# A finished tile's sums and products behind the thresholding pass, a small product and half of a ratio to VectorE

## The chip, the cores and the metric

The kernel runs on one core of a Trainium2 chip. A core has five engines with a queue of instructions each: TensorE (PE; its weight loads are shown as PEld), VectorE (DVE), ScalarE (ACT), GpSimd (POOL) and SyncE (SP), which issues most of the DMAs. Each engine works through its queue in order and waits on semaphores for the others. The metric is the device time of one execution in microseconds, as a median of several runs, here 1416.24 us (1415.47 to 1416.34 in 3 runs).

## The reference

A layer of a graph network on 3327 nodes with 256 features, all in float32. The input is normalized and cut at zero; then there are two steps, each with a fixed diffusion and an attention whose rows keep only the largest probabilities up to a mass of 0.9.

```python
def _top_p_attention(X, W1, W2, W3):
    q = X @ W1.T @ W2.T
    k = X @ W3.T
    probs = jax.nn.softmax(q @ k.T / TAU, axis=-1)
    idx = jnp.argsort(-probs, axis=-1)
    sp = jnp.take_along_axis(probs, idx, axis=-1)
    cs = jnp.cumsum(sp, axis=-1)
    keep_sorted = cs - sp < TOP_P
    mask = ...  # keep_sorted, put back in place
    A = probs * mask
    return A / jnp.maximum(A.sum(-1, keepdims=True), 1e-12)

R = S + jnp.eye(N)
R = R / R.sum(-1, keepdims=True)
for n in range(2):
    A = _top_p_attention(Xa, W1, W2, W3)
    Xf = R @ Xf
    Xa = A @ Xa
    Z = Z + Xf @ U1[n].T + Xa @ U2[n].T
h = X + Z
out = x + (h - mean) / sqrt(var + 1e-5) * ln_g + ln_b
```

## The kernel before

The 3327 nodes are 26 tiles of 128 rows (NT). A first part makes the keys, the products with the weights and the first lists; then come the two steps of the reference, called step 1 and step 2 here (`step` 0 and 1 in the code), tile after tile. At the end a flag says whether every row's cut was proved; if not, a second, slow kernel (`search_graph_layer`) would run. It doesn't for this input.

For one tile of 128 rows the work is:

- `weights`: TensorE makes the logits against all 3328 keys, ScalarE takes the exponential into an array `e` (128x3328).
- `measured_twice` (step 2; `measured_once` in step 1): a guess of the cut that is refined. ScalarE passes over all of `e` three times in step 2 (`through`, the tile `ja`, L633), and each pass ends in one sum per row. Between the passes small columns (128x1, the tile `g`, `col(k)` in the code) are worked out on VectorE, ScalarE and GpSimd. L685 and L686 follow the first pass; L690 to L692 on GpSimd make columns 14, 10 and 8; L699 and L700 follow the second pass; L707 to L712 on GpSimd make the ratio that ends in column 11, which ScalarE's L714 needs. L716 and L717 make the guess, column 16.
- `settle`: VectorE keeps what lies below the guess (L731, the tile `w`, 128x3328), takes the eight largest of each of 20 segments (L736), sorts out the largest in rounds (L743, L745), finds the cut (L750 to L755), masks `e` in place with the row sum beside it (L765) and takes the reciprocal (L766). L767 multiplies two arrays of 48 (40 in step 1) columns into `cum`, and L769 takes its maximum for the proof. L767 is on VectorE in step 1 and on GpSimd in step 2.
- `Sums`: TensorE transposes the masked `e` (L810), ScalarE copies it (L812), TensorE multiplies it with the features (L824).
- `spread`: the diffusion by a few gathered rows (`refetch` issues five gathers on GpSimd, L903; TensorE L911), ended by VectorE's L1086 into `s`.
- `finish` (step 2): L935 on VectorE joins the two sums, L458 and L459 take mean and variance, GpSimd makes the inverse deviation (L465, L466) and L943, ScalarE normalizes (L950), GpSimd adds the offset to the input rows `xr` (L945), multiplies (L951) and adds (L952), and SyncE writes the tile out (L955).

Order: each of these is a Python generator, and a table written by hand says when each takes its next part. Every tile's turn `i` has seven slots; a letter in a slot's string takes one part of one generator: `m` and `n` are the measuring of the next tile and the rest of the one before it, `d` and `c` the same for `settle`, `s` is `spread`, `f` is `finish`, `w` is `weights`, `g` the gathers. The order in which instructions are issued by the program is then fixed on TensorE, ScalarE and VectorE, and in step 2 on GpSimd, by dependencies that need no semaphore. So a part that is moved in the text moves in its engine's queue.

In step 2 GpSimd's queue for a tile is: L707 to L712, L945, L951, L952, L767, L677 and L678 (the next tile's first columns, which wait for ScalarE's L676), five gathers, L690 to L692, L465, L466, L943, L697, L698. On VectorE L717 is followed by L731, L732, L769, ten of L736, L935, L685, L686, L1086, ten more of L736, L458, L459, three rounds, L699, L700, three rounds, L750 to L755, L765, L766, L716, L717.

Of the kernel before, what the change touches and what calls it, by code (L numbers as in the profile page):

```python
# [14 lines left out]
ALU = mybir.AluOpType  # L15
# [7 lines left out]
NT = (N + P - 1) // P  # L23
# [321 lines left out]
def guess_graph_layer(ctx, tc, x, adj, w1t, w2t, w3t, u1t, u2t, ln_g, ln_b, out, flag):  # L345
# [323 lines left out]
    def measured_twice(r):  # L669
        e, ms = r["e"], r["ms"]  # L670

        col = guessed(r, small.tile([P, 18], F32, tag="g", name="g"))
        S.activation(col(1), col(0), AF.Exp, scale=-1.0, bias=con(5))
        S.activation(col(11), col(2), AF.Square, bias=con(4))  # L676
        G.tensor_scalar(col(11), col(11), ms(5), ms(6), ALU.mult, ALU.add)  # L677
        G.tensor_scalar(col(5), col(1), OFFSET[1], None, ALU.mult)  # L678
        yield
        oa = small.tile([P, 3], F32, tag="oa", name="oa")  # L680
        through(e, AF.Relu, col(9), -1.0, oa[:, 0:1])
        yield
        through(e, AF.Sign, col(9), -1.0, oa[:, 1:2])
        yield
        V.tensor_scalar(col(3), oa[:, 1:2], float(NP), col(9), ALU.add, ALU.mult)  # L685
        V.tensor_scalar(col(4), col(3), 0.5, oa[:, 0:1], ALU.mult, ALU.subtract)  # L686
        S.activation(col(6), col(4), AF.Ln, scale=col(1), bias=con(2))
        S.activation(col(6), col(6), AF.Exp, scale=col(11))
        S.activation(col(13), col(6), AF.Copy, scale=col(9))
        G.tensor_scalar(col(14), col(13), col(9), 0.25, ALU.add, ALU.mult)  # L690
        G.tensor_scalar(col(10), col(13), col(5), 1.0, ALU.mult, ALU.add)
        G.tensor_scalar(col(8), col(4), col(1), -1.0, ALU.mult, ALU.add)  # L692
        yield
        through(e, AF.Sign, col(13), -1.0, oa[:, 2:3])
        yield
        d1 = col(17)
        G.tensor_scalar(col(0), oa[:, 2:3], NP - 61.0, BIG, ALU.is_gt, ALU.mult)  # L697
        G.tensor_scalar(col(0), r["Z"], 0.035, col(0), ALU.mult, ALU.add)  # L698
        V.tensor_scalar(col(15), oa[:, 2:3], oa[:, 1:2], col(14), ALU.subtract, ALU.mult)  # L699
        V.tensor_scalar(d1, col(15), col(4), 0.0, ALU.add, ALU.max)  # L700

        S.activation(col(2), d1, AF.Abs, scale=col(1), bias=con(1))
        S.activation(col(2), col(2), AF.Ln, scale=0.2, bias=col(10))
        S.activation(col(3), d1, AF.Ln, scale=col(1), bias=con(2))
        S.activation(col(2), col(2), AF.Identity, scale=-1.0, bias=col(3))

        G.tensor_scalar(col(12), col(4), d1, col(1), ALU.subtract, ALU.mult)  # L707
        G.tensor_scalar(col(8), col(8), col(12), None, ALU.mult)
        G.tensor_scalar(col(12), col(12), col(12), 1.0e-12, ALU.mult, ALU.add)
        G.tensor_tensor(col(12), col(12), half[:, 2:3], ALU.pow)  # L710
        G.tensor_scalar(col(12), col(12), col(8), 0.7, ALU.mult, ALU.max)
        G.tensor_scalar(col(11), col(12), 1.5, col(11), ALU.min, ALU.mult)  # L712
        yield
        S.activation(col(3), col(2), AF.Exp, scale=col(11))  # L714
        yield
        V.tensor_scalar(col(6), d1, col(0), BIG, ALU.is_lt, ALU.mult)  # L716
        V.tensor_scalar(col(16), col(3), col(13), col(6), ALU.mult, ALU.add)  # L717
# [7 lines left out]
    def settle(step, t, r):  # L725
        e, col, Z = r["e"], r["col"], r["Z"]
        n = 8 * ROUNDS[step]
        d2 = small.tile([P, 1], F32, tag="d2", name="d2")
        need = small.tile([P, 1], F32, tag="need", name="need")
        w = scan.tile([P, NP], F32, tag="w", name="w")  # L730
        V.scalar_tensor_tensor(w, e, col(16), e, ALU.is_lt, ALU.mult, accum_out=d2)  # L731
        V.tensor_scalar(need, Z, -0.1, d2, ALU.mult, ALU.add)  # L732
        yield
        cand = small.tile([P, NSEG * 8], F32, tag="cand", name="cand", bufs=1)
        for s in range(NSEG):
            V.max(cand[:, 8 * s : 8 * s + 8], w[:, s * SEG : min(NP, (s + 1) * SEG)])  # L736
            if s in (NSEG // 2 - 1, NSEG - 1):
                yield
        at = lambda k: rec[:, step, k, t : t + 1]
        V.tensor_reduce(at(0), cand.rearrange("p (s k) -> p s k", k=8)[:, :, 7], AX.X, ALU.max)  # L740
        for k in range(ROUNDS[step]):
            b8 = bb[:, 1 + 8 * k : 9 + 8 * k]
            V.max(b8, cand)  # L743
            if k < ROUNDS[step] - 1:
                V.match_replace(cand, b8, cand, 0.0)  # L745
            if k == 2:
                yield
        b = bb[:, 1 : n + 1]
        cum = small.tile([P, TOPK], F32, tag="cum", name="cum", bufs=1)
        V.tensor_tensor_scan(cum[:, :n], bb[:, :n], bb[:, :n], 0.0, ALU.add, ALU.max)  # L750

        dr = small.tile([P, TOPK], F32, tag="dr", name="dr", bufs=1)
        V.tensor_scalar(dr[:, :n], cum[:, :n], need, None, ALU.is_ge)
        V.scalar_tensor_tensor(cum[:, :n], dr[:, :n], BIG, b, ALU.mult, ALU.add)
        V.tensor_reduce(at(1), cum[:, :n], AX.X, ALU.min)  # L755
        yield
        r["ra"] = ra = small.tile([P, 1], F32, tag="ra", name="ra")
        if t in (0, NT - 1):

            rb = small.tile([P, 1], F32, tag="rb", name="rb", bufs=1)  # L760
            for a, b_, r_ in ((0, FIRST, ra), (FIRST, NP, rb)):
                V.scalar_tensor_tensor(e[:, a:b_], e[:, a:b_], at(1), e[:, a:b_], ALU.is_ge, ALU.mult, accum_out=r_)
            V.tensor_tensor(ra, ra, rb, ALU.add)
        else:
            V.scalar_tensor_tensor(e, e, at(1), e, ALU.is_ge, ALU.mult, accum_out=ra)  # L765
        V.reciprocal(ra, ra)  # L766
        (G if step else V).tensor_tensor(cum[:, :n], dr[:, :n], b, ALU.mult)  # L767
        yield
        V.tensor_reduce(at(2), cum[:, :n], AX.X, ALU.max)  # L769


# [162 lines left out]
    def finish(t, y, pa, ra):  # L934
# [7 lines left out]
        nm = small.tile([P, 1], F32, tag="nm", name="nm")  # L942
        G.tensor_scalar(nm, mv[:, 0:1], rstd, -1.0, ALU.mult, ALU.mult)  # L943
        yield
        G.tensor_tensor(xr, xr, bet, ALU.add)  # L945
        if t == NT - 1:
            V.scalar_tensor_tensor(y, y, mv[:, 0:1], gam, ALU.subtract, ALU.mult)
            V.scalar_tensor_tensor(y, y, rstd, xr, ALU.mult, ALU.add)
        else:
            S.activation(y, y, AF.Identity, bias=nm, scale=rstd)  # L950
            G.tensor_tensor(y, y, gam, ALU.mult)  # L951
            G.tensor_tensor(y, y, xr, ALU.add)  # L952
        yield
        h = min(P, N - t * P)
        nc.sync.dma_start(out[t * P : t * P + h], y[:h])  # L955

# [135 lines left out]
    def refetch(t):  # L1092
# [8 lines left out]


    PLAN = (("mdsssa", "mdsssa", "edawwp", "msda", "mpdea", "gdawwq", "emdgq"),
            ("llcmss", "lnms", "lwwnfd", "lcmdsssg", "fmswqdf", "llmdf", "lmwfd"))

    LAST = {NT - 1: ("cfss", "cn", "ndddddd", "sss", "fsf", "f", "f"), NT: ("cf", "v", "", "", "ff", "f", "fv")}
    LATE = (1, 4)
# [122 lines left out]
```

## Time and profile before

| what | value |
|---|---|
| median of 3 runs | 1416.24 us (1415.47 to 1416.34) |
| the profiled execution | 1414.41 us |
| its span in the profile | 1412.7 us |
| granted TensorE clock, mean | 0.973 of full speed |
| busy: PE, DVE, ACT, POOL | 1275.6, 1220.8, 1105.4, 983.1 us |
| step 1 | about 90 to 780 us of the span |
| step 2, from the first full tile to the last | 833 to 1344 us, 23 intervals from mask pass to mask pass |

The profile is one execution. An instruction's line is its place in the code (L765), followed by the engine, the operation, the tile it writes and those it reads, and shapes. In a timeline the first column is the start in us from the span's start and the second the duration in us, from the moment that the engine takes it up; an instruction that is held by something else than a semaphore is shown as long, and the bracket at the end of a line says how long the engine was idle before it and who ended that. A busy share of 90% says little on what sets the time; the waits and the chain that ended last say more.

### The profile page before, as it was taken

To read this page: it belongs to the slowest core of one execution; us is meant where nothing else is said; L and a number is where in the kernel's file an instruction comes from. 1 tells how busy PE (TensorE), PEld (TensorE's weight loads), DVE (VectorE), ACT (ScalarE), POOL (GpSimd) and SP (SyncE) were. 2 spreads that over 40 slices of the span, in tenths; PEclk is the share of its full clock that TensorE was granted. 3 is DMA by queue.
4 is the path that set the end of the run, shared out by engine and by line. 5 is a ranking of instruction groups with operands and counts; after the bars stand their busy time and mean duration, and the time that the engine had idled before them with its cause. 6 is when DMAs were issued, how large, how long until landed. Compare 5 with 4: busy or idle time off the path is not lost.

```text
span 1412.7 us, 22245 instructions
## 1 busy us (share of the span) xinstructions
PE 1275.6 (90%) x6495; PEld 980.1 (69%) x6495; DVE 1220.8 (86%) x3727; ACT 1105.4 (78%) x2423; POOL 983.1 (70%) x1348
## 2 busy tenths in 40 slices
PE   6898999999999999999998479999999999999846
PEld 5545777777777777778786257777777777777745
DVE  6879999999999999998853689999999999999980
ACT  5467887878778787888835689999999999999811
POOL 6214777678667676778853768888888888888721
PEclk9999999999999999999999589999999999999978
DMA  8884454444545454423331211312222122221100
GB/s 273 266 254 127 135 150 130 137 139 141 144 128 147 128 143 144 132 82 91 88 97 49 71 44 54 90 57 79 76 59 87 55 85 59 77 83 53 57 8 22
DMA packets 91203, 149.78 MB, mean 106 GB/s; under 512 B 15265, under 2 KB 58656, under 8 KB 91072
## 3 DMA queue, kind: packets, MB, share of 16 engines
q1 hardware_dynamic: 73616, 105.37, 23.7%
q0 software_dynamic: 16640, 42.69, 11.9%
q8 instruction: 54, 0.88, 0.3%
q14 instruction: 77, 0.63, 0.1%
q10 hardware_dynamic: 816, 0.20, 0.1%
HBM read 120.93 MB, written 27.28 MB: 105 GB/s over the span
## 4 chain that ended last, share of the span: by engine, by line
DVE 51%; PE 25%; ACT 17%; POOL 3%; issue 3%; DMA 1%; SPq 0%; DVEq 0%; POOLq 0%; ACTq 0%
ACT ja L633 11%; PE pa L824 10%; DVE e L765 10%; DVE cand L736 7%; DVE w L731 6%; DVE fm L846 5%; PE pl L600 4%; DVE bb L743 4%; DVE cand L745 4%; PE pt L810 3%; PE pz L988 2%; DVE x L765 2%; ACT eT L812 2%; PE pr L911 1%; ACT e L604 1%
## 5 line engine op out<-in xcount | busy, mean ns | idle before, releaser
L824 PE MATMUL pa<-xw,eT 128*128 128x256 f32 x1352 | 331.1, 387 | 18.6 <-DVE s L935 18.4
L633 ACT ACTIVATE ja<-e,g 128x3328 uint8<-128x3328 f32 x106 | 325.9, 3074 | 0.1
L824 PE MATMUL pa<-x,eT 128*128 128x256 f32 x1352 | 323.7, 381 | 0.0
L824 PEld LDWEIGHTS pa<-xw,eT 128*128 128x128 f32 x1352 | 249.6, 191 | 79.6 <-issue 27.1
L812 ACT COPY eT<-pt 128x512 f32<-128x512 f32 (+1 forms) x364 | 202.1, 556 | 92.9 <-PE pt L810 92.8
L824 PEld LDWEIGHTS pa<-x,eT 128*128 128x128 f32 x1352 | 244.1, 191 | 25.7
L736 DVE MAX8 cand<-w 128x8 f32<-128x168 f32 (+1 forms) x1040 | 251.1, 317 | 0.0
L810 PE MATMUL pt<-ident,e 128*128 128x128 f32 x1144 | 180.6, 278 | 57.9 <-DVE e L765 39.1
L894 POOL DMA_INDIRECT ac<-in_adj,index x130 | 130.2, 1002 | 133.1 <-DVE ms L538 94.9
L903 POOL DMA_INDIRECT xg<-bx,index x130 | 192.4, 1480 | 41.3 <-issue 28.9
L810 PEld LDWEIGHTS pt<-ident,e 128*128 128x128 f32 x1144 | 140.8, 144 | 104.7 <-issue 48.8
L731 DVE SCALAR_TENSOR_TENSOR w<-e,g 128x3328 f32<-128x3328 f32 x44 | 168.9, 3838 | 0.7
L903 POOL DMA_INDIRECT xg<-vx,index x130 | 130.8, 1007 | 45.6 <-issue 33.0
L765 DVE SCALAR_TENSOR_TENSOR e<-e,rec 128x3328 f32<-128x3328 f32 x40 | 156.3, 3907 | 0.7
L911 PE MATMUL pr<-xg,ac 128*128 128x257 f32 (+1 forms) x520 | 139.1, 391 | 11.4 <-DVE s L1086 11.2
L604 ACT ACTIVATE e<-pl 128x832 f32<-128x832 f32 x132 | 112.9, 859 | 36.1 <-PE pl L600 36.0
L911 PEld LDWEIGHTS pr<-xg,ac 128*128 128x128 f32 x520 | 93.9, 195 | 24.9 <-DVE s L1086 11.4
L951 POOL TENSOR_TENSOR s<-s,gam 128x256 f32<-128x256 f32 x25 | 92.5, 3699 | 8.5 <-ACT s L950 8.5
L743 DVE MAX8 bb<-cand 128x8 f32<-128x160 f32 x286 | 92.8, 324 | 6.4
L600 PE MATMUL pl<-after,qT 64*128 64x416 f32 x416 | 96.7, 559 | 0.6 <-ACT qT L528 0.6
L767 POOL TENSOR_TENSOR cum<-dr,bb 128x48 f32<-128x48 f32 x26 | 84.8, 3262 | 15.1 <-DVE rec L755 14.9
L600 PE MATMUL pl<-both,qT 64*128 64x416 f32 x416 | 90.7, 539 | 0.9 <-DVE both L1006 0.9
(259 smaller groups left out, 2197.3 us busy)
## 6 DMA issues: line engine op xcount, KB each, us to landing
at<-in_adj SPq DMA_DIRECT2D x102, 256.0 KB, 3.0
cx<-ac SPq DMA_DIRECT2D x26, 384.0 KB, 2.3
ac<-cx SPq DMA_DIRECT2D x26, 384.0 KB, 3.1
wide<-in_adj SPq DMA_DIRECT2D x10, 832.0 KB, 4.3
e<-in_adj SPq DMA_DIRECT2D x8, 832.0 KB, 5.9
bx<-e SPq DMA_DIRECT2D x26, 128.5 KB, 2.2
own<-bx SPq DMA_DIRECT2D x26, 128.5 KB, 2.9
x<-in_x SPq DMA_DIRECT2D x13, 256.0 KB, 4.7
```

The source lines that it names most:

```text
L600: PE.matmul(pl[:, a, :wd], qT[p, :], keys_of(step, a).rearrange("p a b -> p (a b)")[:, c : c + wd], start=True, stop=True)
L633: S.activation(ja, e, f, bias=guess, scale=sign, accum_out=total)
L731: V.scalar_tensor_tensor(w, e, col(16), e, ALU.is_lt, ALU.mult, accum_out=d2)
L736: V.max(cand[:, 8 * s : 8 * s + 8], w[:, s * SEG : min(NP, (s + 1) * SEG)])
L743: V.max(b8, cand)
L765: V.scalar_tensor_tensor(e, e, at(1), e, ALU.is_ge, ALU.mult, accum_out=ra)
L810: PE.transpose(pt[:, j, :], e[:, (j0 + j) * P : (j0 + j + 1) * P], ident)
L812: S.copy(eT[:, :w, :], pt[:, :w, :])
L824: PE.matmul(self.pa, eT[:, c - 4 * k, :], self.xa[:, j, :], start=c == 0, stop=c == NT - 1)
L894: G.indirect_dma_start(out=ac[:, k, :], out_offset=None, in_=rows, in_offset=bass.IndirectOffsetOnAxis(ap=index[:, t, k : k + 1], axis=0), ...
L903: G.indirect_dma_start(out=xg[:, k, :w], out_offset=None, in_=rows, in_offset=bass.IndirectOffsetOnAxis(ap=index[:, t, k : k + 1], axis=0))
L911: PE.matmul(pr[:, :w], ac[:, k, :], own if k == KT - 1 else xg[:, k, :w], start=k == 0, stop=k == KT - 1)
```

## The change

There are four edits.

1. In `measured_twice` the ratio is worked out in another form. Column 8 is now column 4 less a tenth of `Z` (still one GpSimd instruction). Column 12 is the reciprocal of column 4 less `d1`, by two VectorE instructions, in place of four on GpSimd (a difference with a product, a product, a square with an offset, a power of -1). The last two GpSimd instructions stay.
2. In `settle` the product `cum` is on VectorE in both steps, and it is issued one part later, directly ahead of the maximum that reads it. In step 1 it was on VectorE already.
3. In `finish` the three GpSimd instructions on a finished tile come one part later, so that in GpSimd's queue they stand behind L677 and L678 of the next tile and ahead of the gathers. The writing out, which waits for them, stays behind them. The last tile is as it was.
4. In the table's fifth slot of step 2 `fmswqdf` becomes `fsmwqdf`: on VectorE L1086 comes directly ahead of L685 and L686.

```diff
-        G.tensor_scalar(col(8), col(4), col(1), -1.0, ALU.mult, ALU.add)
+        G.tensor_scalar(col(8), r["Z"], -0.1, col(4), ALU.mult, ALU.add)
...
-        G.tensor_scalar(col(12), col(4), d1, col(1), ALU.subtract, ALU.mult)
-        G.tensor_scalar(col(8), col(8), col(12), None, ALU.mult)
-        G.tensor_scalar(col(12), col(12), col(12), 1.0e-12, ALU.mult, ALU.add)
-        G.tensor_tensor(col(12), col(12), half[:, 2:3], ALU.pow)
+        V.tensor_scalar(col(12), col(4), d1, 1.0e-30, ALU.subtract, ALU.add)
+        V.reciprocal(col(12), col(12))
         G.tensor_scalar(col(12), col(12), col(8), 0.7, ALU.mult, ALU.max)
         G.tensor_scalar(col(11), col(12), 1.5, col(11), ALU.min, ALU.mult)
...
         V.reciprocal(ra, ra)
-        (G if step else V).tensor_tensor(cum[:, :n], dr[:, :n], b, ALU.mult)
-        yield
+        yield
+        V.tensor_tensor(cum[:, :n], dr[:, :n], b, ALU.mult)
         V.tensor_reduce(at(2), cum[:, :n], AX.X, ALU.max)
...
         yield
-        G.tensor_tensor(xr, xr, bet, ALU.add)
         if t == NT - 1:
+            G.tensor_tensor(xr, xr, bet, ALU.add)
             V.scalar_tensor_tensor(y, y, mv[:, 0:1], gam, ALU.subtract, ALU.mult)
             V.scalar_tensor_tensor(y, y, rstd, xr, ALU.mult, ALU.add)
         else:
             S.activation(y, y, AF.Identity, bias=nm, scale=rstd)
+        yield
+        if t < NT - 1:
+            G.tensor_tensor(xr, xr, bet, ALU.add)
             G.tensor_tensor(y, y, gam, ALU.mult)
             G.tensor_tensor(y, y, xr, ALU.add)
-        yield
         h = min(P, N - t * P)
         nc.sync.dma_start(out[t * P : t * P + h], y[:h])
...
-            ("llcmss", "lnms", "lwwnfd", "lcmdsssg", "fmswqdf", "llmdf", "lmwfd"))
+            ("llcmss", "lnms", "lwwnfd", "lcmdsssg", "fsmwqdf", "llmdf", "lmwfd"))
```

## The prediction

> **What bounds the kernel now.** I read the page first: its busy times and the shares of the chain that ended last.
>
> ```profile
> span 1412.7 us, 22245 instructions
> PE 1275.6 (90%) x6495; PEld 980.1 (69%) x6495; DVE 1220.8 (86%) x3727; ACT 1105.4 (78%) x2423; POOL 983.1 (70%) x1348
> DVE 51%; PE 25%; ACT 17%; POOL 3%; issue 3%; DMA 1%; SPq 0%; DVEq 0%; POOLq 0%; ACTq 0%
> ```
>
> VectorE (DVE) leads the chain and GpSimd (POOL) holds only 3% of it, so time taken off GpSimd pays only where GpSimd holds up another engine. Most edits lie in step 2, so next I read who waits there: VectorE's waits from 820 to 1340 us (sum in us, times, longest).
>
> ```profile
> engine line waited for: us in total, times, longest us
> DVE g L685 <- ACT ja L633: 11.0, 22, 0.9
> DVE g L699 <- ACT ja L633: 7.8, 20, 3.4
> ```
>
> Once per tile VectorE waits for each of two ScalarE passes. Following them in time gives one closed loop per tile: first pass (ja) ends, L685 and L686, ScalarE's L687, second pass, L699 and L700, the rest of the candidate rounds, the mask pass L765 (e, 128x3328), TensorE's transposes, ScalarE's copy of them, first pass of the next tile. A tile takes 22.2 us. What is added on this loop adds to every tile; the thresholding pass L731 (w) is beside it, with the wait at L685 as its slack. The timeline of VectorE (start, duration, both in us) shows what GpSimd does to it. First a tile without a collision, then usual ones:
>
> ```profile
> 833.29 3.69 DVE L765 SCALAR_TENSOR_TENSOR e<-e,rec 128x3328 f32<-128x3328 f32 x1
> 837.71 3.68 DVE L731 SCALAR_TENSOR_TENSOR w<-e,g 128x3328 f32<-128x3328 f32 x1
> 844.03 0.47 DVE L935 SCALAR_TENSOR_TENSOR s<-pa,ra,s 128x256 f32<-128x256 f32 x1
> 845.43 0.21 DVE L685 TENSOR_SCALAR g<-oa,g 128x1 f32<-128x1 f32 x1 [0.94 <-ACT ja L633]
> 855.11 4.07 DVE L765 SCALAR_TENSOR_TENSOR e<-e,rec 128x3328 f32<-128x3328 f32 x1
> ...
> 1033.10 4.08 DVE L765 SCALAR_TENSOR_TENSOR x<-x,rec 128x3328 f32<-128x3328 f32 x1
> 1037.91 4.13 DVE L731 SCALAR_TENSOR_TENSOR w<-x,g 128x3328 f32<-128x3328 f32 x1
> 1045.63 0.21 DVE L685 TENSOR_SCALAR g<-oa,g 128x1 f32<-128x1 f32 x1 [0.48 <-ACT ja L633]
> ```
>
> and GpSimd's own timeline beside 1033 us:
>
> ```profile
> 1032.96 0.72 POOL L945 TENSOR_TENSOR xr<-xr,bet 128x256 f32<-128x256 f32 x1
> 1033.66 4.10 POOL L951 TENSOR_TENSOR s<-s,gam 128x256 f32<-128x256 f32 x1
> 1037.84 0.72 POOL L952 TENSOR_TENSOR s<-s,xr 128x256 f32<-128x256 f32 x1
> 1038.52 3.65 POOL L767 TENSOR_TENSOR cum<-dr,bb 128x48 f32<-128x48 f32 x1
> ```
>
> A GpSimd product that started 0.14 us before L765 makes it 4.08 instead of 3.69; one that started 0.07 before L731 makes that 4.13. Over all tiles the delay is about 0.52 us less the head start. The next GpSimd instruction is then held until the pass ends (4.10 and 3.65 for work of 0.72 and 0.26). The tile that starts undelayed at 833.29 lasts 21.82 us to the next L765, against 22.2: the 0.40 is on the loop.
>
> **The change, part by part.** All terms are against the profiled execution, 1414.41 us (span 1412.7 and 1.7 around it), which is 1.83 below the median 1416.24.
>
> *L765 set free.* The three instructions on a finished tile (L945, L951, L952) now stand behind L677 and L678, which wait for ScalarE's L676; that ends some 2 us after L765 starts. GpSimd is idle when L765 starts: 22 tiles times 0.40 = -8.8 us.
>
> *Half of the last ratio to VectorE.* Four GpSimd instructions go (L707 to L710, 0.37+0.29+0.26+0.57); L711 and L712 stay. VectorE gains a subtraction and a reciprocal behind L700, each waiting for the one before. A dependent pair of this form has a pitch of 0.25 (L685 to L686), L700 to an independent successor 0.13, L766's reciprocal to its successor 0.08: 0.25+0.25+0.08-0.13 = 0.45 us, on the loop, because L699 is released by ScalarE and idle time before it cannot be used. 23 pitches times 0.45 = +10.4. The bound below is 0.16+0.08 = 0.24, if the two overlap as independent ones do; above 0.60. I take 0.45, whose rows have the same form. L702 to L705 on ScalarE wait for L700 only and don't move. L692 keeps its one instruction in a new form, 0.25 either way.
>
> [...]
>
> *The sums and products in their new place.* L677 is held by L765 until 0.14 before its end, as other held instructions are; then 0.41 to L678, 0.23 to the sum: 4.17 us after L765's start. L731 starts 4.42 after it (833.29 to 837.71). So the sum is in flight with a head start of 0.25, and L731 is delayed by 0.52-0.25 = 0.27 instead of 0.45. The product is held by L731 and runs when it ends, where the next edit puts a two-input VectorE instruction. The writing out of the tile (SyncE) moves from 5.5 to about 10 us behind L765; behind it in that queue stand x, s, ac and own of later tiles, first used 15 us or more after. GpSimd's five gathers follow the product at about 9.7; today they start at 10.0, held by TensorE. I cost both at nothing; gathers late by over a microsecond would reach L697.
>
> [...]
>
> *cum to VectorE, s in front of L685.* In step 2 cum costs VectorE 0.22 (in step 1 one tile already has the pair adjacent: 724.78 to 725.00), and 0.27 more if the product is in flight: the same pair collides in step 1, where the source view has durations (ns, least, median, most)
>
> ```profile
> L767 DVE TENSOR_TENSOR cum<-dr,bb x26: 179/181/522, 116.3 to 724.8; 128x40 f32<-128x40 f32 x26
> ```
>
> L1086 (0.40) moves from behind L686 to before L685. The slack there without collisions is 845.43-844.43 = 1.00. After: 1.00-0.40-0.22-0.27 (L731)-0.27 (cum) = -0.16, so L685 is late by 0.16 instead of waiting. 23 times 0.16 = +3.7. Bounds: 0 (either collision absent) and 0.34 (L731 delayed by 0.45 as today).
>
> *Irregular tiles.* At 899.5 and 1055.3 gathers came late, and pitches were 22.54 and 23.05; GpSimd now has over 1 us more room: -1.1.
>
> *Step 1.* cum moves five rows back. It leaves a place where it costs 0.10, to one where it costs 0.22 as half of an adjacent pair: 26 times 0.12 = +3.1, on an engine that hardly waits there. At ten tiles it cost 0.44 instead of 0.10, behind L928; the new place is about 1.5 us later, when L928 is over: -3.4. Together -0.3, bounds -3 and +3.
>
> *The start and the end of step 2.* These are the places where GpSimd is waited for.
>
> ```profile
> 811.30 0.29 ACT L714 ACTIVATE g<-g 128x1 f32<-128x1 f32 x1 [0.77 <-POOL g L712]
> ...
> 1350.04 0.20 DVE L769 TENSOR_REDUCE rec<-cum 128x1 f32<-128x48 f32 x1 [1.44 <-POOL cum L767]
> ```
>
> At the start the ratio ends about 1.3 us earlier for tile 0 and 2.1 for tile 1, of which 0.45 comes back in VectorE: -1.6 at 833 us. At the end L731 starts 6.45 after L765; without the wait and the collision it is 3.73 to the reciprocal and 1.03 from there (0.08, cum 0.22, 0.12, 0.30, 0.31) = 4.76: -1.7, less 0.2 for a possible collision: -1.5.
>
> The sum: -8.8+10.4+3.7-1.1-0.3-1.6-1.5 = +0.8 us. On the median: 1417.0.
>
> **The rivals.** About 0.2% (2.8 us) is what a measurement here can tell from no change.
>
> *Faster: the slack holds.* If GpSimd's sum starts after L731 rather than 0.25 before, or cum is not hit, the 3.7 disappears: -2.9. With the two new instructions at 0.30 instead of 0.45 another -3.4: 1410 to 1413.3. For it: the head start of 0.25 is a difference of two chains. Against: the held instruction is released by L765's end, which fixes the order.
>
> *Slower: VectorE becomes the loop at L685.* If L731 is still delayed by 0.45, L685 is 0.34 late, another 0.18 times 23 = +4.1: 1421.1, and with step 1 at its upper bound (+3.3 on mine) 1424.4. It decides from 0.09 of lateness beyond mine in each tile (2.0 us). For it: 0.34 of delay was measured for cum in step 1. Against: L731's delay has always followed the head start.
>
> *It frees nothing: GpSimd is hidden anyway.* Only the loop's 0.45 would then stay; excluded for L765, since the 21.82 pitch is in the trace, and possible if GpSimd's gathers drift until L711 and L712 meet L765: up to 8.8 more, 1425.8.
>
> **How the numbers follow.** Forecast (terms nearly cancel) 0.45; faster rival 0.24; slower rival 0.26; nothing freed 0.05. The forecast's own range is 1413.5 to 1419; towards the rivals 1411 to 1424.5, with about 0.1 beyond each end. Within 0.2% of 1416.24 is 1413.4 to 1419.1: the forecast case, with a little of it lost to each side and a little of the rivals gained. Faster 0.25, same 0.44, slower 0.31.
>
> **What would show it.** In the profile after, step 2: the mask pass at 3.68 in all tiles; the w pass near 3.95; cum near 0.5; no wait left at the L685 of today, one of 0.6 or more at L699; pitch of a tile 22.35 to 22.5; the last w pass 4.8 after the mask pass; ScalarE's L714 not waiting for GpSimd. Step 1: cum 0.18 everywhere. I am wrong if the mask pass still shows 4.08, if the pitch is under 22.2 or over 22.6, or if the gathers start over 1 us later than today.

## The result and the profile after

| | kernel before | changed kernel |
|---|---|---|
| median, same chip, 20 runs each | 1415.91 us (1414.01 to 1417.81) | 1417.85 us (1415.57 to 1421.31) |
| ratio, 95% interval | | 1.0017 [1.0011, 1.0023] |
| the profiled execution | 1414.41 us | 1416.86 us |
| start to last mask pass of step 1 | 700.58 | 699.19 |
| from there to the first mask pass of step 2 | 132.71 | 130.69 |
| 23 intervals of step 2 | 511.04 | 518.11 |
| last mask pass to the end of the span | 68.37 | 67.11 |
| usual pitch of a tile in step 2 | 22.20 | 22.51 |

The changed kernel is 0.17% slower. Step 2's loop lost 7.1 us; step 1, the start and the end of step 2 gave 4.7 back. The code of the changed kernel is two lines shorter in places, so the lines have moved: the mask pass is L763 (was L765), w L729 (L731), need L730 (L732), cum L766 on VectorE (L767 on GpSimd), its maximum L767 (L769), L935 is L933, the ratio's two GpSimd instructions L709 and L710 (L711, L712), the sum and products of a finished tile L951 to L953. L677, L678, L685, L699, L700 and L1086 stay. The page after, as quoted of before (span, busy times, shares of the chain that ended last):

```profile
span 1415.1 us, 22191 instructions
PE 1279.0 (90%) x6495; PEld 980.5 (69%) x6495; DVE 1229.4 (87%) x3805; ACT 1105.9 (78%) x2423; POOL 892.3 (63%) x1218
DVE 58%; PE 24%; ACT 11%; issue 3%; POOL 2%; DMA 1%; SPq 0%; DVEq 0%; POOLq 0%; ACTq 0%
```

GpSimd is busy for 91 us less, and the time didn't fall: 78 instructions went to VectorE, whose share of the chain rose from 51% to 58%. VectorE's waits from 820 to 1340 us (sum in us, times, longest) say in which place:

```profile
DVE g L699 <- ACT ja L633: 13.7, 20, 1.8
...
DVE g L685 <- ACT ja L633: 0.3, 1, 0.3
```

The wait at L685, 22 times and 11.0 us before, is gone but for the first tile. VectorE now comes too late there. The timeline of VectorE in a usual tile, from one mask pass to the next (start, duration, in us):

```profile
1009.71 3.68 DVE L763 SCALAR_TENSOR_TENSOR e<-e,rec 128x3328 f32<-128x3328 f32 x1
1014.13 4.06 DVE L729 SCALAR_TENSOR_TENSOR w<-x,g 128x3328 f32<-128x3328 f32 x1
1018.37 0.47 DVE L766 TENSOR_TENSOR cum<-dr,bb 128x48 f32<-128x48 f32 x1
1021.74 0.47 DVE L1086 SCALAR_TENSOR_TENSOR s<-pr,rrs,s 128x256 f32<-128x256 f32 x1
1022.13 0.20 DVE L685 TENSOR_SCALAR g<-oa,g 128x1 f32<-128x1 f32 x1
1028.37 0.27 DVE L699 TENSOR_SCALAR g<-oa,g 128x1 f32<-128x1 f32 x1 [0.63 <-ACT ja L633]
1028.68 0.21 DVE L700 TENSOR_SCALAR g<-g 128x1 f32<-128x1 f32 x1
1028.92 0.21 DVE L707 TENSOR_SCALAR g<-g 128x1 f32<-128x1 f32 x1
1029.17 0.16 DVE L708 RECIPROCAL g<-g 128x1 f32<-128x1 f32 x1
...
1032.22 3.68 DVE L763 SCALAR_TENSOR_TENSOR x<-x,rec 128x3328 f32<-128x3328 f32 x1
```

and GpSimd beside it:

```profile
1012.05 1.56 POOL L677 TENSOR_SCALAR g<-g,law 128x1 f32<-128x1 f32 x1 [4.42 <-ACT g L676]
1013.70 0.23 POOL L678 TENSOR_SCALAR g<-g 128x1 f32<-128x1 f32 x1
1013.99 0.73 POOL L951 TENSOR_TENSOR xr<-xr,bet 128x256 f32<-128x256 f32 x1
1014.67 4.11 POOL L952 TENSOR_TENSOR s<-s,gam 128x256 f32<-128x256 f32 x1
1018.86 0.73 POOL L953 TENSOR_TENSOR s<-s,xr 128x256 f32<-128x256 f32 x1
...
1029.43 0.30 POOL L709 TENSOR_SCALAR g<-g 128x1 f32<-128x1 f32 x1 [0.47 <-DVE g L708]
1029.84 0.30 POOL L710 TENSOR_SCALAR g<-g 128x1 f32<-128x1 f32 x1
```

Four things are to be read here. The mask pass is free of GpSimd (3.68 instead of 4.08). The sum L951 is in flight, by 0.14 us, when the w pass starts at 1014.13, and the pass takes 4.06 instead of 3.69; the product L952, held until that pass is nearly over, meets cum at 1018.37, which takes 0.47 instead of 0.20. L685 stands 12.42 us behind the mask pass with no wait in front of it; in the tile that waited there it came at 12.14. And L700, L707, L708 start 0.24 and 0.25 apart, on the loop.

### The profile page after: what moved, and what is told of

The parts are those of the page before. It is cut to its first block, busy times and chain, and to the rows that moved or that the text cites. A ratio compares the mean times of both kernels' runs of the same rounds, so it can differ in the third digit from the quotient of the medians.

```text
span 1415.1 us, 22191 instructions
## 1 busy us (share of the span) xinstructions
PE 1279.0 (90%) x6495; PEld 980.5 (69%) x6495; DVE 1229.4 (87%) x3805; ACT 1105.9 (78%) x2423; POOL 892.3 (63%) x1218
## 4 chain that ended last, share of the span: by engine, by line
DVE 58%; PE 24%; ACT 11%; issue 3%; POOL 2%; DMA 1%; SPq 0%; DVEq 0%; POOLq 0%; ACTq 0%
DVE w L729 11%; PE pa L822 10%; DVE cand L734 10%; DVE e L763 9%; ACT ja L633 6%; DVE fm L844 5%; DVE bb L741 4%; DVE cand L743 3%; PE pl L600 3%; PE pt L808 3%; DVE x L763 2%; PE pz L988 2%; PE pr L909 2%; PE pz L922 1%; DVE s L1086 1%
## 5 line engine op out<-in xcount | busy, mean ns | idle before, releaser
L892 POOL DMA_INDIRECT ac<-in_adj,index x130 | 133.5, 1027 | 124.8 <-DVE ms L538 86.2
L729 DVE SCALAR_TENSOR_TENSOR w<-e,g 128x3328 f32<-128x3328 f32 x44 | 168.4, 3826 | 0.7
L763 DVE SCALAR_TENSOR_TENSOR e<-e,rec 128x3328 f32<-128x3328 f32 x40 | 149.6, 3741 | 0.7
L677 POOL TENSOR_SCALAR g<-g,law 128x1 f32<-128x1 f32 x23 | 36.3, 1580 | 99.4 <-ACT g L676 99.4
L952 POOL TENSOR_TENSOR s<-s,gam 128x256 f32<-128x256 f32 x25 | 92.6, 3703 | 9.0 <-ACT s L948 9.0
```

The costliest lines, as they stand in the source:

```text
L892: G.indirect_dma_start(out=ac[:, k, :], out_offset=None, in_=rows, in_offset=bass.IndirectOffsetOnAxis(ap=index[:, t, k : k + 1], axis=0), ...
```

## The experiments

The theory was that a tile's pitch is one closed loop with three separate terms: 0.39 us gained at the mask pass, some 0.42 lost to the two new VectorE instructions, 0.28 lost by lateness at L685. The rivals: that undoing one term only shows the next wait, that the collisions with GpSimd's products cost nothing beside L1086's move, or that the clock or transfers set the time. In each run the four stretches of the table are compared from the profiles, since whole times on the chips of the experiments spread more (step 1 alone, from its first to its last mask pass, took 562 to 579 us in profiles whose step 1 is the same text but for cum's place). The ratios below come with 95% intervals. On the chips where the runs spread most they differ from the quotient of the two medians by up to 0.4% (0.9961 against 0.9998 with only cum back), so there the pitch in the profile carries the argument, and the ratio doesn't.

**Only L1086 back behind L685 and L686.** The rest as in the changed kernel.

```diff
-  "fsmwqdf", "llmdf", "lmwfd"
+  "fmswqdf", "llmdf", "lmwfd"
```

> The changed kernel with the table's slot as it was before (L1086 behind L686 again). My theory: in step 2 of the changed kernel VectorE comes to L685 0.28 us late in every tile (12.42 us behind the mask pass instead of the 12.14 at which ScalarE is ready), because three things are now ahead of it: L1086 (0.40), cum with its collision (0.51) and the delay of the w pass (0.38). Taking L1086 away leaves 12.03, so L685 waits for ScalarE again, and L1086 fits into the 0.63 of idle time ahead of L699. Interval between mask passes 22.51 down to 22.23, 22 tiles: about -6.2 us against the changed kernel, 0.997 of the kernel before. Rival: the slot fills a wait as it is meant to, and without it the 0.40 of L1086 lands on the loop ahead of L699: interval 22.5 to 22.9, 1.002 to 1.008 of the kernel before.

Measured: pitch 22.25, 0.26 less; L685 at 12.14, with w still at 4.06 and cum at 0.48. Ratio to the kernel before 0.9988 [0.9963, 1.0012]; 23 intervals 514.71, in spite of one of 22.84 and a last one of 24.60.

```profile
1011.06 3.69 DVE L763 SCALAR_TENSOR_TENSOR e<-e,rec 128x3328 f32<-128x3328 f32 x1
1015.48 4.06 DVE L729 SCALAR_TENSOR_TENSOR w<-x,g 128x3328 f32<-128x3328 f32 x1
...
1023.20 0.21 DVE L685 TENSOR_SCALAR g<-oa,g 128x1 f32<-128x1 f32 x1
...
1033.31 3.69 DVE L763 SCALAR_TENSOR_TENSOR x<-x,rec 128x3328 f32<-128x3328 f32 x1
```

The collisions alone still fit into L685's slack; with the 0.40 of L1086 ahead of it they no longer do. So the third term is the fourth edit's, given the collisions.

**Only the ratio back on GpSimd.**

```diff
-  V.tensor_scalar(col(12), col(4), d1, 1.0e-30, ALU.subtract, ALU.add)
-  V.reciprocal(col(12), col(12))
+  G.tensor_scalar(col(12), col(4), d1, col(1), ALU.subtract, ALU.mult)
+  G.tensor_scalar(col(8), col(8), col(12), None, ALU.mult)
+  G.tensor_scalar(col(12), col(12), col(12), 1.0e-12, ALU.mult, ALU.add)
+  G.tensor_tensor(col(12), col(12), half[:, 2:3], ALU.pow)
...
-  G.tensor_scalar(col(8), r["Z"], -0.1, col(4), ALU.mult, ALU.add)
+  G.tensor_scalar(col(8), col(4), col(1), -1.0, ALU.mult, ALU.add)
```

> The changed kernel with the last ratio as it was before, all of it on GpSimd (column 8 too). My theory: the two VectorE instructions behind L700 are worth 0.45 us on the loop of every tile: interval 22.51 down to 22.06, 23 times -0.45 = -10.4 us, and some 1.5 to 2 us come back at the start of step 2, where ScalarE waits for the ratio: about 1409.5, 0.9955 of the kernel before. GpSimd's chain L707 to L712 then ends about 0.1 us ahead of the mask pass and isn't held, except in tiles whose gathers are late. Rival: that chain is held by the mask pass in most tiles (L711 or L712 at 3.6 us), ScalarE's Exp waits for it and each such tile loses 0.8: interval 22.9, 1.008 of the kernel before. A third: the two instructions are hidden, interval stays 22.5.

Measured: pitch 22.09, 0.42 less; L699 still after 0.64. 23 intervals 511.41 with two long tiles, 22.42 and 24.08 near 1031 to 1078, and a last one of 23.44; the stretch ahead of step 2's first mask pass 134.60, 3.9 longer. The pitch is as expected; the ratio, 0.9979 [0.9955, 1.0003], missed the 0.9955, since 3.9 instead of 1.5 to 2 us came back at the start and the long tiles were not reckoned with. The two dependent instructions of 0.21 and 0.16 cost the loop 0.42.

**Only the sum and products back in their old place.**

```diff
   S.activation(y, y, AF.Identity, bias=nm, scale=rstd)
+  G.tensor_tensor(xr, xr, bet, ALU.add)
+  G.tensor_tensor(y, y, gam, ALU.mult)
+  G.tensor_tensor(y, y, xr, ALU.add)
   yield
-  if t < NT - 1:
-      G.tensor_tensor(xr, xr, bet, ALU.add)
-      G.tensor_tensor(y, y, gam, ALU.mult)
-      G.tensor_tensor(y, y, xr, ALU.add)
```

> The changed kernel with the three GpSimd instructions on a finished tile in their old place, ahead of L677. My theory: with the shorter ratio chain they no longer meet the mask pass as before: the sum is done early, the product starts when ScalarE has normalized the tile, 0.5 us ahead of the mask pass, so that pass is delayed by 0.05 at most (3.74 us), the last sum is held and runs when the mask pass ends, 0.9 ahead of the w pass, which is free (3.69), and so is cum (0.22). L685 is not late: interval 22.51 down to 22.28, -5 us, 0.998 of the kernel before. Rival: the new place is what sets the mask pass free; in the old one it is delayed by 0.40 again and that is on the loop: interval 22.63 or more, 1.0035 of the kernel before.

Measured: w 3.68 and cum 0.20, but the mask pass 3.84 to 3.86 and the pitch 22.40. I had expected the pass to be nearly free and 22.28; this was wrong by 0.12. The shorter ratio lets the product start earlier, 0.37 ahead of the pass:

```profile
1223.96 0.72 POOL L950 TENSOR_TENSOR s<-s,gam 128x256 f32<-128x256 f32 x1 [1.03 <-ACT s L948]
```

```profile
1224.33 3.84 DVE L763 SCALAR_TENSOR_TENSOR e<-e,rec 128x3328 f32<-128x3328 f32 x1
```

The delay is 0.16, and 0.52-0.37 = 0.15: the head-start rule of the prediction holds at a third place. Ratio 0.9991 [0.9963, 1.0018], against 0.998 expected; 23 intervals 518.99, with long ones of 23.10, 24.14 and 24.04.

**Only cum back on GpSimd in step 2.**

```diff
+  if step: G.tensor_tensor(cum[:, :n], dr[:, :n], b, ALU.mult)
   yield
-  V.tensor_tensor(cum[:, :n], dr[:, :n], b, ALU.mult)
+  if not step: V.tensor_tensor(cum[:, :n], dr[:, :n], b, ALU.mult)
```

> The changed kernel with the small product cum back on GpSimd in step 2 (step 1 as in the changed kernel). My theory: cum is then held by the mask pass and runs at its end; L677, L678 and the sums come 0.4 later, behind the start of the w pass, which is therefore free (3.69), and VectorE is rid of 0.51 (cum and its collision): L685 waits for ScalarE again, interval 22.51 down to 22.23, about -6 us against the changed kernel, 0.997 of the kernel before. Gathers start up to 1 us later and may cost in single tiles. Rival: the lateness at L685 is not due to cum and the w pass; interval stays at 22.5, 1.0017 of the kernel before.

Measured: pitch 22.24, w 3.69, L685 at 12.14 after 0.54, 23 intervals 511.47, ratio 0.9961 [0.9935, 0.9987]. Held on GpSimd by the mask pass (as at 833.34 in the kernel before, where it takes 3.76), cum pushes L677, L678 and the sum back; the sum comes 0.10 behind the start of w, and w is free. The sum starts 0.24 us later than in the changed kernel, and the tile is 0.27 shorter. But here cum's 0.47 has left VectorE too, so this run alone doesn't show that the later start is enough. If it is, any small instruction should do it:

**One GpSimd instruction more.**

```diff
   G.tensor_scalar(col(5), col(1), OFFSET[1], None, ALU.mult)
+  G.tensor_scalar(col(7), col(1), OFFSET[1], None, ALU.mult)
```

> The changed kernel with one GpSimd instruction more in each tile of step 2: L678's column (128x1, 0.23 us) is computed a second time into an unused column, between L678 and the sum of offset and input. Theory (what delays the thresholding pass is the sum in flight when it starts): the sum now comes about 0.1 us after the pass has started, is held until its end and delays it by at most 0.15; the pass takes 3.69 to 3.8 instead of 4.06, cum may still show 0.48 or a little more. L685 then comes at 12.14 after the mask pass, as ScalarE releases it, instead of 12.42, and the pitch is 22.25 instead of 22.51: more work makes the tile shorter, 1412 to 1414 where the changed kernel's profile had 1416.9. Rival (the products behind the pass delay it wherever they stand, or more work in GpSimd's queue just costs): w stays at 4.06 or more, the pitch at 22.51 or longer, the time 1417 or more.

Measured: w 3.69 in every tile, pitch 22.24. The timelines of VectorE and of GpSimd (the lines have moved by one here: L730 is w, L767 cum, L952 the sum):

```profile
1017.55 3.69 DVE L764 SCALAR_TENSOR_TENSOR e<-e,rec 128x3328 f32<-128x3328 f32 x1
1021.98 3.69 DVE L730 SCALAR_TENSOR_TENSOR w<-x,g 128x3328 f32<-128x3328 f32 x1
1025.83 0.47 DVE L767 TENSOR_TENSOR cum<-dr,bb 128x48 f32<-128x48 f32 x1
...
1039.80 3.69 DVE L764 SCALAR_TENSOR_TENSOR x<-x,rec 128x3328 f32<-128x3328 f32 x1
```

```profile
1021.83 0.21 POOL L679 TENSOR_SCALAR g<-g 128x1 f32<-128x1 f32 x1
1022.10 4.14 POOL L952 TENSOR_TENSOR xr<-xr,bet 128x256 f32<-128x256 f32 x1
```

The sum comes 0.12 behind the start of w and is held instead of holding. More work makes the usual tile 0.27 shorter. The whole time didn't follow: five intervals of this profile are long (23.65, 23.89, 23.15, 23.12, 24.14), so that the 23 take 518.27, and the ratio is 1.0022 [1.0000, 1.0043], against an expectation of 1412 to 1414 us. In those of 23.89 and 24.14 the granted clock was one half for 3.4 us, and in that of 23.12 the gathers came 2.5 late, as in the same tile of the changed kernel; why the two of 23.65 and 23.15 are long I did not settle. So the run shows the shorter tile, and no faster kernel.

**Without the sum and products.**

```diff
-  if t < NT - 1:
-      G.tensor_tensor(xr, xr, bet, ALU.add)
-      G.tensor_tensor(y, y, gam, ALU.mult)
-      G.tensor_tensor(y, y, xr, ALU.add)
```

> The changed kernel without the three GpSimd instructions on a finished tile (all tiles but the last): the output lacks the factor and the offset of the last normalization and the addition of the input in those tiles. Theory (L685's lateness is the sum of two collisions with them and of L1086's move): w 3.69, cum 0.20, L685 released by ScalarE at 12.14 after a wait of about 0.38 (0.28 late less 0.38 and 0.28 of collisions), pitch 22.24, the same 22.25 that came from undoing L1086's move alone. Rival (the collisions cost nothing beside L1086's move): the pitch stays near 22.5. Rival (GpSimd's products cost the loop elsewhere too, for instance at L699 or in the writing out): the pitch falls below 22.2.

Measured: w 3.69, cum 0.20, L685 at 12.14 after 0.30, pitch 22.24, 23 intervals 510.73, ratio 0.9993 [0.9973, 1.0013] (step 1 took 568.6 us in this profile, 4.4 more than in that of the changed kernel). The wait of 0.30 is counted from the end of L1086 (L1082 there), 0.48 after its start; in the changed kernel L685 follows that start by 0.39, so it is 0.39 early here. From 0.28 late to 0.39 early is 0.67, near the two collisions of 0.38 and 0.27. The pitch doesn't fall below 22.24: beyond these collisions the three instructions cost a usual tile nothing. The last interval is 21.57, against 22.99 with them.

**Ratio and L1086 both back, products and cum as changed.** The first two diffs of this section together.

> The changed kernel with the ratio back in its old form on GpSimd and with L1086 back behind L686; the products and cum stay moved. Theory (the two losses are separate terms on one loop): pitch 22.51-0.26-0.43 = 21.82, as in the tile without a collision of the kernel before; the start of step 2 as in the run with the ratio alone put back (the stretch from the last mask pass of step 1 to the first of step 2 is 134 against 130.7), an irregular tile where GpSimd's gathers come late: 23 intervals near 505 against 518.1, 1405 to 1410 in all, a ratio to the kernel before of 0.993 to 0.997. Rival (the two share one slack, so that undoing one takes most of what the other gives): pitch 22.0 to 22.1 and a ratio of 0.997 or more.

Measured: pitch 21.82, as added up from the single runs.

```profile
1145.70 3.69 DVE L765 SCALAR_TENSOR_TENSOR e<-e,rec 128x3328 f32<-128x3328 f32 x1
...
1167.52 3.69 DVE L765 SCALAR_TENSOR_TENSOR x<-x,rec 128x3328 f32<-128x3328 f32 x1
```

23 intervals 506.26, near the expected 505, the start 134.76; 1412.10 us as the median of 7 runs, over the expected 1405 to 1410, where the kernel before has 1418.75 on the same chip, ratio 0.9934 [0.9905, 0.9962]. The terms are separate; no shared slack.

**The same, with the short ratio kept in the first two tiles and the last.**

```diff
+  r["edge"] = t in (0, 1, NT - 1)
...
+  if r["edge"]:
+      V.tensor_scalar(col(12), col(4), d1, 1.0e-30, ALU.subtract, ALU.add)
+      V.reciprocal(col(12), col(12))
+  else:
+      G.tensor_scalar(col(12), col(4), d1, col(1), ALU.subtract, ALU.mult)
...
```

> As the run with the ratio and L1086 both put back, but the first two tiles and the last of step 2 keep the changed kernel's ratio on VectorE, where GpSimd was waited for. Theory: pitch 21.82 in the middle, the start as in the changed kernel (130 to 132 against 134), the end at 67: 2 to 4 us below the run with the ratio back everywhere, 1402 to 1407, a ratio to the kernel before of 0.990 to 0.994. Rival (the start is set by something else than the ratio, transfers or the clock): no difference from the run with the ratio back everywhere.

Measured: pitch 21.83, the start 132.76 instead of 134.76, 2.0 shorter though not the expected 130 to 132; but irregular tiles of 22.85, 25.21 and 24.46, the last two with the clock at one half for 3.4 us, 23 intervals 509.77, ratio 0.9951 [0.9931, 0.9971], where 0.990 to 0.994 was expected. The 2 us at the start are there, and not to be seen in the time.

**The third edit alone, on the kernel before.**

```diff
-  G.tensor_tensor(xr, xr, bet, ALU.add)
   if t == NT - 1:
+      G.tensor_tensor(xr, xr, bet, ALU.add)
...
       S.activation(y, y, AF.Identity, bias=nm, scale=rstd)
-      G.tensor_tensor(y, y, gam, ALU.mult)
-      G.tensor_tensor(y, y, xr, ALU.add)
   yield
+  if t < NT - 1:
+      G.tensor_tensor(xr, xr, bet, ALU.add)
+      G.tensor_tensor(y, y, gam, ALU.mult)
+      G.tensor_tensor(y, y, xr, ALU.add)
```

> The kernel before with the third edit alone: the three GpSimd instructions on a finished tile stand behind L677 and L678; ratio, cum and the slots as before. Theory (this edit alone makes the gain, the others only take from it in the loop): mask pass 3.69; cum, held on GpSimd by the mask pass, pushes the sum behind the start of the thresholding pass, so w 3.69 too; L685 at 12.14 after a wait of 0.9 to 1.0; L699 at 18.40 after 0.24; pitch 21.82; the start of step 2 and its end as in the kernel before (last mask pass of step 1 to first of step 2 about 133, from the last mask pass to the end about 68); one or two irregular tiles. 23 intervals 503 to 507 against 511.0 and 518.1; 1406 to 1411, a ratio to the kernel before of 0.993 to 0.997. Rival (the moved products need the room that the shorter ratio makes on GpSimd): gathers a microsecond or more late, L699 waiting for GpSimd, pitch 22.0 or more and a ratio of 0.998 or more.

Measured: mask 3.69, w 3.69, L685 at 12.14 after 0.93, L699 at 18.39 after 0.23, pitch 21.81; 1407.23 us against 1414.73, ratio 0.9949 [0.9937, 0.9962]. VectorE's timeline of a usual tile:

```profile
1120.55 3.69 DVE L765 SCALAR_TENSOR_TENSOR e<-e,rec 128x3328 f32<-128x3328 f32 x1
1124.96 3.69 DVE L731 SCALAR_TENSOR_TENSOR w<-e,g 128x3328 f32<-128x3328 f32 x1
1132.68 0.21 DVE L685 TENSOR_SCALAR g<-oa,g 128x1 f32<-128x1 f32 x1 [0.93 <-ACT ja L633]
1142.35 3.69 DVE L765 SCALAR_TENSOR_TENSOR e<-e,rec 128x3328 f32<-128x3328 f32 x1
```

One of the four edits makes the whole gain of the loop. 23 intervals take 507.51, just over the expected 503 to 507, for three tiles of 22.71, 24.01 and 23.45. GpSimd's timeline shows where the second comes from, a usual tile first and then that one:

```profile
1120.47 0.30 POOL L712 TENSOR_SCALAR g<-g 128x1 f32<-128x1 f32 x1
```

```profile
1041.39 1.12 POOL L903 DMA_INDIRECT xg<-vx,index  x1 [2.63 <-PE pq L523]
...
1051.34 3.70 POOL L709 TENSOR_SCALAR g<-g 128x1 f32<-128x1 f32 x1
...
1056.20 0.30 POOL L712 TENSOR_SCALAR g<-g 128x1 f32<-128x1 f32 x1
```

In a usual tile the old ratio's last instruction starts at 1120.47, 0.08 before the mask pass at 1120.55. Where the gathers came 2.5 late, after a wait of 2.63, L709 of the ratio met the mask pass at 1051.28 and was held for 3.70; ScalarE waited 2.31 for L712 and the w pass started 5.89 behind the mask pass instead of 4.42. With the old ratio the same instruction is held in the tile behind those gathers in all four profiles that have the old ratio there with moved products. In the changed kernel that tile is 22.82 and the next is usual, since its ratio ends 2.1 us ahead of the mask pass (1029.84+0.30 against 1032.22). So the short ratio should be worth its 0.42 in that one tile:

**The third edit, and the short ratio in tiles 0, 1, 12 and 25 only.**

```diff
+  r["short"] = t in (0, 1, 12, NT - 1)
...
+  if r["short"]:
+      V.tensor_scalar(col(12), col(4), d1, 1.0e-30, ALU.subtract, ALU.add)
+      V.reciprocal(col(12), col(12))
+  else:
...
```

> The kernel before with the third edit, and with the changed kernel's ratio on VectorE in four tiles of step 2 only: 0 and 1, where ScalarE waited for GpSimd's ratio at the start, 12, whose ratio ran into the mask pass at 1051 us with the third edit alone (one GpSimd instruction of it held 3.70), and the last. Theory (the shorter ratio pays where GpSimd's queue is late and costs 0.43 elsewhere): pitch 21.81 in the middle; behind the late gathers one tile of 22.7 to 23.2, and the two that followed it at 24.01 and 23.45 become 21.8; the start 131 to 133 against 133.2. 23 intervals 502.5 to 505 against 507.5, 1400 to 1404, a ratio to the kernel before of 0.990 to 0.9935. Rival (the tiles behind the late gathers are slow for another reason, the TensorE clock above all): the two long tiles stay, and the ratio stays at 0.994 to 0.996.

Measured: the tile behind the late gathers 23.14, the next two 21.85 and 21.84, the start 131.80; ratio 0.9930 [0.9900, 0.9959] on a chip where the kernel before took 1429.88. Its 23 intervals took 506.67, not the expected 502.5 to 505, because the old ratio's last instruction met the mask pass in three other tiles too (held 3.75 to 3.77; 22.56, 22.63, 22.56). Its interval overlaps that of the third edit alone: which of the two is faster is open.

**cum back in its old place in step 1 only, and the changed kernel again on that chip.**

```diff
   V.reciprocal(ra, ra)
+  if not step: V.tensor_tensor(cum[:, :n], dr[:, :n], b, ALU.mult)
   yield
-  V.tensor_tensor(cum[:, :n], dr[:, :n], b, ALU.mult)
+  if step: V.tensor_tensor(cum[:, :n], dr[:, :n], b, ALU.mult)
```

> The changed kernel with cum in its old place in step 1 (behind the reciprocal of the row sum, ahead of the yield), and on VectorE in its new place in step 2. Theory: cum shows 0.5 instead of 0.19 at about ten tiles of step 1 as before, VectorE hardly waits there, so that step 1 becomes 1 to 3 us longer than that of the changed kernel on the same chip, in a spread of several us from run to run; step 2 as in the changed kernel, pitch 22.51; ratio to the changed kernel 1.000 to 1.002. Rival (step 1 has become longer by the move, by the 0.12 that cum costs as half of an adjacent pair): step 1 becomes 1 to 3 us shorter.

> The changed kernel itself, to have it on the chip of these runs. Pitch 22.51, 23 intervals 517 to 520, a ratio to the kernel before of 0.999 to 1.003. If step 1 sets the difference between chips, its last mask pass comes 0 to 15 us later than at 699 us and the stretch behind it stays within 3 us of the first profile.

Measured: from the first mask pass of step 1 to the last 565.13 with cum in the old place and 563.91 in the new (565.71 and 564.28 in the profiles of before and after). In the old place the source view (ns: least, median, most) has the collisions of before:

```profile
L766 DVE TENSOR_TENSOR cum<-dr,bb x26: 178/182/521, 115.9 to 723.8; 128x40 f32<-128x40 f32 x26
```

The changed kernel's ratio on this chip is 1.0023 [1.0013, 1.0032], with pitch 22.51 and 518.08 for the 23 intervals; with cum in the old place 1.0047 [1.0034, 1.0059]. Step 1 alone doesn't make up the 2.65 us between the two medians (1420.47 and 1417.82): in the profiles the start of step 2 is 1.2 longer with the old place, where the clock was at one half for 44.4 instead of 41.0 us of that stretch, and the last interval 1.6, also by the clock (see the end), while the stretch ahead of step 1 is 2.7 shorter. The step-1 term would be 1.2 us, but from one profile of each: on another chip four profiles with the same step 1 took 562.4 to 579.1 us, so that cum's place is its cause is not shown. The rest is not explained by the edit.

## Why the prediction came out

The forecast was 1417.0 us and no measurable change, the result 1417.85 and a ratio of 1.0017, just inside 0.2%. Against its own sum, step by step, in us over the kernel (measured per tile times 23, or 22 for the first):

| step | predicted | measured | from |
|---|---|---|---|
| mask pass set free | -8.8 | -8.6 | 22.20 to 21.81 with the third edit alone |
| half of the ratio on VectorE | +10.4 | +9.7 | 22.51 to 22.09 without it |
| cum and s ahead of L685 | +3.7 | +6.0 | 22.51 to 22.25 with s behind |
| irregular tiles and the last interval | -1.1 | 0.0 | rest of the 23 intervals, 7.07 |
| step 1 | -0.3 | -1.4 | 700.58 to 699.19 |
| start of step 2 | -1.6 | -2.0 | 132.71 to 130.69 |
| end | -1.5 | -1.3 | 68.37 to 67.11 |
| sum | +0.8 | +2.4 | profiles: 1414.41 to 1416.86 |

*The mask pass and the two VectorE instructions* were right in mechanism and size. The loop shows 0.42 of the 0.45. The pitch of 0.24 to 0.25 for a dependent instruction decided the sign: without the 9.7 that the two cost, the 23 intervals would by this table be 2.6 us shorter than before, where they are 7.1 longer.

*Lateness at L685* was right as a mechanism and mis-sized: "the sum is in flight with a head start of 0.25", and so a delay of 0.27. It was 0.14 and 0.38. From L678 to the sum it took 0.29 and not 0.23, and L678 came 0.05 later, 3.99 behind the mask pass; a difference of two chains of 4.2 us each was off by 0.11, and that is 0.11 times 23 = 2.5 us. The rule itself, 0.52 less the head start, held: 0.38 at 0.14, 0.16 at 0.37 where it gives 0.15, and none where the sum starts 0.12 behind the pass (w 3.69, one instruction more). At the start of the pass the sum had 0.73-0.14 = 0.59 left to run, and the pass was delayed by 0.38 only. cum's collision was right (0.27 more).

By its own terms the loop thus went to the slower rival's side: that was to decide from 0.09 of lateness beyond mine, and it was 0.12. What kept the forecast is step 1, the ratio and the start, 1.1, 0.7 and 0.4 better than reckoned, against 1.1 lost in the row of irregular tiles and the last interval. That they made up for it is luck: no step of the sum foresaw it, and without the 1.1 of step 1 the two medians would be about 3.0 us apart, more than the 2.8 that counted as no change.

*Step 1.* The prediction charged cum's new place with 0.12 for each of 26 tiles against 3.4 saved on collisions. Both are there. The collisions are gone (cum's 26 instructions take 4.93 us instead of 8.08), and from cum's start to the next instruction it is 0.23 in nearly every tile, where it was 0.10 or, in ten tiles, 0.44: 5.86 us in all instead of 6.10, so -0.2 on VectorE, near the -0.3 forecast. Yet step 1 is 1.4 shorter, and 1.2 between the two kernels that differ in nothing else. cum's time on VectorE explains only -0.2 of the one and -0.6 of the other; where the rest comes from stays open.

*Irregular tiles.* The long tiles of 22.54 and 23.05 became one of 22.82: their excess over the pitch fell by 0.9, with 1.1 forecast. But the last interval, which the prediction had no step for, went from 21.79 to 22.99. Behind the last tile but one no L677 holds the products back, and they run unheld at 1345.12 to 1347.43, beside L748 and L751, which take 0.55 and 0.70 instead of 0.26 and 0.25. These 0.74, with the 0.38 at w and the 0.27 at cum, are 1.39, near the 1.42 by which this interval is shorter without the three instructions.

*Start and end* were right in mechanism: L712 on ScalarE (L714 before) no longer waits for GpSimd (0.09 and nothing for the first two tiles, 1.40 and 0.77 before), and the last w pass starts 4.77 after the mask pass, with 4.76 forecast. The size at the start is less sure than the table looks, since the clock differs too: it was at one half for 44.4 us of that stretch before and for 41.0 after. The two runs whose half clock is the same there, 44.4 us, and which differ in the ratio of the first two tiles and the last, are 2.0 apart at the start.

*That it frees nothing* is refuted by the third edit alone: 0.39 a tile. Its other half, gathers that drift until the ratio meets the mask pass, doesn't happen in the changed kernel, and happened, in one to three tiles, in every kernel that has the products moved and the old ratio. The prediction priced it as a rival for the changed kernel only, and not as the margin of 2 us that the short ratio buys.

## What to carry to other kernels

Moving an instruction paid here where it met another engine's long pass on the loop: one edit out of four made the loop's gain, 0.39 us a tile, and others took it back through 0.4 us on a loop that runs 23 times. Work out where a moved instruction starts to a tenth of a microsecond from both chains, and if the two are that near, put it clearly on one side; one small instruction did so here, for 0.27 us a tile, though the kernel with it was not faster. Compare stages, not only whole times: the stretches showed terms of 0.1 us a tile where the medians showed 0.2%.

## What the runs showed of the hardware

TensorE's clock made the last interval of step 2 vary between kernels with the same pitch. There PE waits 2.0 to 2.9 us for L933. The changed kernel's PE timeline, and then that of the kernel with only L1086 back:

```profile
1337.16 1.99 PE L822 MATMUL pa<-xw,eT 128*128 128x256 f32 x8 [2.93 <-DVE s L933]
```

```profile
1335.33 3.60 PE L822 MATMUL pa<-xw,eT 128*128 128x256 f32 x8 [2.93 <-DVE s L933]
```

The wait is the same, the eight matmuls take 1.99 and 3.60. The windows view of the second (stretch, its length and PE's busy time, granted clock, DMA share, GB/s) has the reason:

```profile
1333.00:1335.00 2.00, 0.00 (x0) 1.00 0.36 106
1335.00:1337.00 2.00, 1.67 (x4) 0.55 0.29 91
1337.00:1339.00 2.00, 2.00 (x8) 0.60 0.00 0
1339.00:1341.00 2.00, 2.00 (x13) 1.00 0.00 0
```

The granted clock fell to one half for about 3.4 us ((0.45+0.40) times 2.00 over one half; with cum back in step 1 the stretch from 1340 to 1342 lies wholly in such a fall and shows 0.50). The last interval is 24.60 here. With one pitch, 22.51, it is 24.54 with cum back in step 1, where the clock fell, and 22.98 in the changed kernel on the same chip, where it did not. With the third edit alone a wait of 1.97 at 1079 was followed by the same loss (a granted clock of 0.92 and 0.65 in the stretches of 4.00 from 1076 and 1080, again 3.4 us at one half). In each profile the stretches of half clock start whole multiples of 3.41 us apart (in that of the kernel before at 773.10, 786.75 and 807.23, 4 and 6 times 3.41 apart). Cut into stretches of that length, the second kernel has PE busy for 0.18 of 1331.78 to 1335.19, and the half clock follows; in the changed kernel the same wait is split over two stretches, with PE busy for 0.54 and 0.60, and none follows. Over this last interval nine of the fourteen profiles have a stretch with PE busy for 0.16 to 0.40 (about 0.21 with cum back in step 1, 0.25 with the short ratio in the first two tiles and the last, 0.40 with it in four tiles), and the half clock comes next in all nine; in the other five no stretch is under 0.46 (0.47 in the kernel before), and the clock stays full. So in this interval the half clock came after stretches that were not wholly idle, and waits of 2 to 3 us were enough where most of one fell into a single stretch. More than that is not shown: in the kernel before the half clock also came after the stretch from 769.68, with PE busy for 0.68.
